# Four-layer image kernel: output projection folded into the value weights, denominators by DMA, half-height copies of left-over channels in the patch stage

## The chip, the cores and the metric

The kernel runs on one core of a Trainium2 chip. The metric is the device time of one execution in microseconds (us), taken as the median of several runs. Everything is computed in float32. Engines are called as in the profile: PE (matrix), PEld (its weight loads), DVE (vector), ACT (scalar), POOL (GpSimd) and SP (which here only issues DMAs).

## What is computed

One image `x` of 48 channels and 128 x 128 pixels goes through four layers, each of the form `x = x + layer(groupnorm(x))`. The change touches layers 0 and 2.

```python
# layer 0: attention over all 16384 pixels, one head of 48 channels
qkv = einsum('bchw,oc->bohw', x, qkv_w)            # 1x1
qkv = depthwise_conv3x3(qkv, dw_w)                 # SAME
q, k, v = split(qkv, 3);  q, k = l2norm(q), l2norm(k)
attn = softmax(einsum('bnc,bmc->bnm', q, k) * temperature)
out = einsum('bnm,bmc->bnc', attn, v)
return einsum('bchw,oc->bohw', out, proj_w)        # the projection

# layer 1: four sweeps of a recurrent 5-tap convolution over rows and columns
# layer 2: the patch stage
hidden = conv1x1(x, w_hidden)                      # 48 -> 288
q, k, v = split(depthwise_conv3x3(hidden, w_dw), 3)
out = irfft2(rfft2(patches(q)) * rfft2(patches(k)))   # 8x8 patches
return conv1x1(v * layernorm_over_channels(out), w_out)
# layer 3: a state-space scan over 4096 tokens of 192 channels
```

## The kernel before

The four layers run one after the other, with the image held in two large SBUF tiles, `xa` and `xb`. Instructions are placed by a scheduler that keeps every dependence; where the source uses the wrapper `InOrder` (ACT and PE in most stages), the order is the one in which the source writes them.

**Layer 0, first part (`attention`).** The 1x1 product and the 3x3 convolution are one matrix product: the weights of `l0_w` and `l0_dw` are multiplied into a tile `wt` (L106 `packed_weights`), whose 128 partitions hold 64 channels of one image row and 64 of the next, and whose last plane takes the left-over channels from a tile `rest`. In `wt` the columns 0 to 127 make q and k and the columns 128 to 191 make v. The groupnorm statistics of `x` (32 `bn_stats`, L155) come first; then bands of 16 rows are normalised, copied by DMA and convolved. Each token's v is turned by PE and stored in `v`, 64 columns per token of which column 32 is set to one (L273), so that the sums below also give the softmax denominator.

**Layer 0, second part (`attend`).** For each of 32 chunks of 512 queries (`c`) and each of 64 key tiles (`j`, both halves of the keys at once), PE makes the scores in four 64 x 64 quarters (`scores`, 4 products), ACT takes the exponential (`e`), and PE sums `v` against it in four quarters (`sums`, 4 products into `acc`). The sums lag the scores by two tiles. PSUM holds three score buffers `s` and one `acc`. When a chunk's sums are complete, `Finish.__init__` copies `acc` to SBUF on ACT (`o`) and adds its halves on DVE (`osum`, L361). Six tiles later `Finish.result` runs: a PE product of `proj` (128 x 112) with `osum` into one of the three `s` buffers, which adds the two key halves, applies the projection and spreads the denominator row over 48 rows; an ACT copy `y`; a DVE reciprocal (L369), a product (L370), the residual added (L371), statistics for the next groupnorm (L372) and a store of 48 x 512 values to `x1` (L373). A second version, `attend_shifted`, stands in the other branch of an `If` and does not run at this temperature.

**Layer 2 (`patch_conv`).** The image is convolved in groups `g` of four rows (32 groups). `fill(r)` prepares eight rows from row `r`: a memset of ones, the normalised rows (`normalise`, L93), one DMA of 49 partitions that shifts the rows by one into the upper half of `xp` (L765), two DMAs of 15 partitions (L768) and six DMAs of 19 partitions (L778, three horizontal shifts for each of two halves) that copy the last 19 channels of the row below into `rest`. For each group, `columns(g)` does three PE products per row from `xp`, `others(g)` a fourth per row from `rest`: even rows read the lower half of `rest` (partitions 0 to 56), odd rows the upper half (64 to 120). After that come the Fourier products (`keys`, `queries`, `back`), the layer norm and gate, and `turn`/`leave`. `rest` has three buffers of eight rows of 130 values. `fill(0)` issues its six `rest` DMAs from ACT, all later fills from SP; `fill(0)` and `fill(8)` stand ahead of the loop, the others are called at every second group.

The kernel lets a DMA go only when the one that last used its completion semaphore has landed; eight such semaphores are used in turn, by SP and ACT together.

Of the kernel before, what the change touches and what calls it, by code (L numbers as in the profile page):

```python
# [19 lines left out]
F32 = mybir.dt.float32  # L20
# [6 lines left out]
C = 48  # L27
H = W = 128
N = H * W
CH = 512  # L30
GAP = 49
# [59 lines left out]
def normalise(nc, out, in_, stats):  # L91
    mean, rstd = stats
    nc.vector.tensor_scalar(out, in_, mean, rstd, ALU.subtract, ALU.mult)  # L93


def rows(ap, n=W):
    return ap.rearrange("c (r w) -> c r w", w=n)


def packed_weights(nc, pool, name, w, dw, cols):  # L100

    w1 = pool.tile([128, 4, cols], F32, name="w1")
# [11 lines left out]
def attention(ctx, tc, xq, other, x1, const, ins):  # L114


    nc = tc.nc
    ident, blk, st = const["ident"], const["blk"], const["st"]
# [3 lines left out]
    kv = ctx.enter_context(tc.tile_pool(name="l0_kv", bufs=1))  # L122

    k = other[:, 0:HALF]

    v = other[:, HALF:N].rearrange("p (t c) -> p t c", c=64)


    proj = kv.tile([128, 64 + C], F32, name="proj")
    nc.vector.memset(proj, 0.0)  # L130
    for b in (0, 64):
        nc.sync.dma_start(proj[b : b + GAP, 0:C], ins["l0_proj"])
        nc.vector.memset(proj[b + 32 : b + 33, 64:], 1.0)
    temp = kv.tile([128, 1], F32, name="temp")
    nc.sync.dma_start(temp, ins["l0_temp"].to_broadcast([128, 1]))

# [3 lines left out]
    absT = kv.tile([128, 1], F32, name="absT")  # L140
    nc.vector.tensor_mul(absT, temp, sgn)

    with ExitStack() as a:
        act, pe = InOrder(tc, nc.scalar), InOrder(tc, nc.tensor)
        wp = a.enter_context(tc.tile_pool(name="l0_w", bufs=1))
        sp = a.enter_context(tc.tile_pool(name="l0_a", bufs=2))
        ps = a.enter_context(tc.tile_pool(name="l0_aps", bufs=4, space=PSUM))
        ps2 = a.enter_context(tc.tile_pool(name="l0_aps2", bufs=2, space=PSUM))
        ps1 = a.enter_context(tc.tile_pool(name="l0_aps1", bufs=1, space=PSUM))


        wt = packed_weights(nc, wp, "wt", ins["l0_w"], ins["l0_dw"], 192)

        for i in range(NQ):
            nc.vector.bn_stats(st[:, i, :], xq[0:C, i * CH : (i + 1) * CH])  # L155
        stats = group_stats(nc, wp, ps2, const, name="pss")
# [5 lines left out]
        rests = [wp.tile([128, R, S], F32, name=f"rest{i}") for i in range(2)]  # L162
# [72 lines left out]
        def take(t0, p, pv):  # L235

            sqs, psss, nrms = [], [], []
            for n in range(2):
                sqs.append(sp.tile([128, CH], F32, name="sq"))
                act.activation(sqs[n], p[n], AF.Square)  # L240
            vt = sp.tile([128, CH], F32, name="vt")
            act.copy(vt, pv)

            for n in range(2):
                psss.append(ps2.tile([128, CH], F32, name="pss"))
                pe.matmul(psss[n], lhsT=blk, rhs=sqs[n], start=True, stop=True)
                nrms.append(sp.tile([128, CH], F32, name="nrm"))
                act.activation(nrms[n], psss[n], AF.Sqrt)
            pt = ps1.tile([128, 4, 2, 64], F32, name="pt")
            for i in range(4):  # L250
                pe.transpose(
                    pt[:, i].rearrange("t n c -> t (n c)"), vt[:, i * 128 : (i + 1) * 128], ident
                )
            kb = 64 * (t0 // HALF)
            tk = t0 % HALF
            left = []
            for n in range(2):
                nc.vector.tensor_scalar_max(nrms[n], nrms[n], 1e-12)
# [13 lines left out]
            nc.gpsimd.memset(k[kb + 32 : kb + 33, tk : tk + 2 * CH], 1.0)  # L272
            nc.gpsimd.memset(v[:, t0 // 128 : t0 // 128 + 8, 32:33], 1.0)  # L273
            return left

        cur = band(0)
# [17 lines left out]
    small = nc.values_load(absT[0:1, 0:1].bitcast(mybir.dt.int32))  # L294
    bits = int(np.float32(32.0).view(np.int32))
    with tc.If(small <= bits) as near:
        attend(tc, xq, k, v, x1, proj, absT, st, ins)
    with near.Else():
        attend_shifted(tc, xq, k, v, x1, proj, absT, ident, st, ins)


@with_exitstack
def attend(ctx, tc, xq, k, v, x1, proj, absT, st, ins):

# [4 lines left out]
    nc = tc.nc  # L309
# [40 lines left out]
    class Finish:  # L350


        def __init__(self, c, acc):
            self.c = c
            self.cols = slice(c * CH, (c + 1) * CH)
            self.xres = sp.tile([C, CH], F32, name="xres")
            nc.sync.dma_start(self.xres, ins["x"][:, self.cols])
            o = sp.tile([128, 2, CH], F32, name="o")
            act.copy(o, acc)
            self.o = sp.tile([128, CH], F32, name="osum")  # L360
            nc.vector.tensor_add(self.o, o[:, 0], o[:, 1])  # L361

        def result(self):
            p = ps_s.tile([128, 2, CH], F32, name="s")[0 : 64 + C, 0, :]
            pe.matmul(p, lhsT=proj, rhs=self.o, start=True, stop=True)
            y = sp.tile([64 + C, CH], F32, name="y")
            act.copy(y, p)
            rec = sp.tile([C, CH], F32, name="rec")
            nc.vector.reciprocal(rec, y[64 : 64 + C])  # L369
            nc.vector.tensor_mul(rec, y[0:C], rec)  # L370
            nc.vector.tensor_add(xq[0:C, self.cols], rec, self.xres)  # L371
            nc.vector.bn_stats(st[:, self.c, :], xq[0:C, self.cols])  # L372
            nc.sync.dma_start(x1[:, self.cols], xq[0:C, self.cols])  # L373

    waiting, finish, acc = [], None, None
    for c in range(NQ):
        for j in range(KT):
# [4 lines left out]
            while len(waiting) > BEHIND:  # L382
                n, i, e = waiting.pop(0)
# [10 lines left out]


@with_exitstack
def attend_shifted(ctx, tc, xq, k, v, x1, proj, absT, ident, st, ins):

    nc = tc.nc
    NQ = N // CH  # L400
# [11 lines left out]
    k16 = k16p.tile([128, HALF], F16, name="k16")  # L412
    for i in range(0, HALF, 2048):
        nc.vector.tensor_copy(k16[:, i : i + 2048], k[:, i : i + 2048])

    class Shift:

# [45 lines left out]
    class Finish:  # L463
# [9 lines left out]

        def result(self):
            p = ps_1.tile([128, CH], F32, name="pmisc")
            nc.tensor.matmul(p[0 : 64 + C], lhsT=proj, rhs=self.o, start=True, stop=True)
            rec = sp.tile([C, CH], F32, name="rec")
            nc.vector.reciprocal(rec, p[64 : 64 + C])
            nc.vector.tensor_mul(rec, p[0:C], rec)
            nc.vector.tensor_add(xq[0:C, self.cols], rec, self.xres)  # L480
            nc.vector.bn_stats(st[:, self.c, :], xq[0:C, self.cols])
            nc.sync.dma_start(x1[:, self.cols], xq[0:C, self.cols])
# [213 lines left out]
def patch_conv(ctx, tc, xq, other, const, ins):  # L696
# [42 lines left out]

    K1 = C + 1
    SP = W + 2
    RN = 8
# [5 lines left out]
    for at in (0, W + 1):  # L750
        nc.gpsimd.memset(xp[:, 1 : H + 1, at : at + 1], 0.0)
    stats = group_stats(nc, wp, ps_f, const, name="f")
    flat = xp.rearrange("c h w -> c (h w)")
    rests = [wp.tile([128, RN, SP], F32, name=f"rest{i}") for i in range(3)]

    def rest(y):

        return rests[(y + 1) // RN % 3][:, (y + 1) % RN, 0:W]

    def fill(r, queue=nc.sync):  # L760
        inside = xp[0:64, 1 + r : 1 + RN + r, 1 : W + 1]
        nc.gpsimd.memset(inside[32:64], 1.0)
        normalise(nc, inside[0:C], rows(xq[0:C, r * W : (r + RN) * W]), stats)
        new = slice(r + 1, r + 1 + RN)
        nc.sync.dma_start(xp[64 : 64 + K1, r : r + RN, :], xp[0:K1, new, :])  # L765
        lo, hi = max(r - 1, 0), H if r + RN == H else r - 1 + RN
        for n in range(2):
            nc.sync.dma_start(  # L768
                xp[64 * n + K1 : 64 * n + 64, lo:hi, :],
                xp[M * n : M * n + M, lo + 2 : hi + 2, :],  # L770
            )
        e = rests[r // RN % 3].rearrange("c h w -> c (h w)")
        size = KR // 3
        long = RN * SP - 2
        for n in range(2):
            for dx in range(3):
                at = 64 * n + size * dx
                queue.dma_start(  # L778
                    e[at : at + size, 0:long],
                    flat[2 * M : K1, (r + 1) * SP + dx : (r + 1) * SP + dx + long],  # L780
                )

    pcs, qkv, prod, lns, ys, yts = {}, {}, {}, {}, {}, {}
# [115 lines left out]
        dve.bn_stats(const["st"][:, g, :], xq[0:C, g * CH : (g + 1) * CH])  # L899

    NG = H // G
    fill(0, act)
    fill(RN)
    for g in range(NG + 3):

# [810 lines left out]
```

## Time and profile before

Three runs took 7662.93, 7664.13 and 7669.04 us; the median is 7664.13. The profiled execution took 7668.22 us, of which 7666.4 lie between the first and the last instruction (the span).

| stage (us of the span) | length | PE busy | what it is |
|---|---|---|---|
| 0 to 43 | 43 | 0.7 | loads, statistics, first band of layer 0 |
| 43 to 254 | 211 | 200.5 | convolution of layer 0 |
| 254 to 3817 | 3563 | 3562.7 | `attend`, 32 chunks |
| 3817 to 3841 | 24 | 2.0 | last result, start of the sweeps |
| 3841 to 4508 | 667 | most | sweeps of layer 1 |
| 4508 to 4560 | 52 | 21.2 | start of the patch stage |
| 4560 to 4880 | 320 | 316.6 | patch stage, steady |
| 4960 to 7667 | 2707 | 1453.3 | scan of layer 3; DVE 2590.7 busy, POOL 2573.7 |

A row of the profile names the line, engine, operation, the tiles written and read, the shape, and the number of instructions that were merged into it. A float32 product appears as two instructions (two passes). The line numbers of products and of most ACT and DVE operations in ordered stages are those of the wrapper (L48), so these are followed by the names of their tiles. "Idle before <- X" is the time that an engine stood still before an instruction, and what ended it.

### The profile page before, as it was taken

The page shows a single profiled execution, that of the slowest core. Times are in us where ns is not written, and L with a number is a line of the kernel's source. Part 1 is how long each engine was busy: PE and PEld are TensorE (multiplying, and loading weights), DVE is VectorE, ACT ScalarE, POOL GpSimd, SP SyncE. Part 2 cuts the span into 40 slices and gives each one's busy share as a digit, 9 for nine tenths or more (in the row PEclk, how much of TensorE's full clock was granted, in tenths as well). Part 3 has the DMA queues.
Part 4 walks back from the last instruction along what each step waited for, and adds up shares of the span by engine and source line. Part 5 has one row for each costly group of instructions (what it writes and reads, how often), then busy time and mean ns, then how long its engine had stood idle before and what let it go on. Part 6 is the DMA issues. An engine that isn't in the chain of part 4 may idle for free. (4 is left out here: it accounts for less than half of the span.)

```text
span 7666.4 us, 202951 instructions
## 1 busy us (share of the span) xinstructions
PE 6186.0 (81%) x93744; PEld 3145.7 (41%) x93744; DVE 3353.1 (44%) x2435; ACT 4405.6 (57%) x4864; POOL 2793.6 (36%) x573
## 2 busy tenths in 40 slices
PE   7999999999999999999988879745545555554555
PEld 2333333333333333333367755434434333434444
DVE  8300000000000000000022234489999999999998
ACT  2566666666666666666625003366666666666665
POOL 1000000000000000000000022299999999999998
PEclk9999999999999999999999999866767666776666
DMA  5000000000000000000000001166556566666776
GB/s 76 10 3 3 3 2 3 3 3 2 3 3 2 3 3 3 2 3 3 6 1 17 1 27 50 31 168 165 158 161 164 152 161 155 164 158 162 181 178 152
DMA packets 167594, 488.77 MB, mean 64 GB/s; under 512 B 33568, under 2 KB 51968, under 8 KB 163984
## 3 DMA queue, kind: packets, MB, share of 16 engines
q1 hardware_dynamic: 160584, 469.79, 24.4%
q8 instruction: 736, 12.06, 0.7%
q10 hardware_dynamic: 6152, 5.92, 0.3%
q14 instruction: 122, 1.00, 0.0%
HBM read 428.82 MB, written 22.02 MB: 59 GB/s over the span
## 5 line engine op out<-in xcount | busy, mean ns | idle before, releaser
L48 ACT ACTIVATE e<-s,absT 128x1024 f32<-128x1024 f32 x2048 | 2279.4, 1115 | 1215.1 <-PE s L48 1215.0
L1471 POOL TENSOR_TENSOR h<-du,bt 128x3072 f32<-128x3072 f32 (+1 forms) x386 | 2559.8, 6670 | 94.5 <-DMA du<-rep 77.4
L48 PE MATMUL s<-xa,xb 49*64 49x512 f32 x16384 | 2127.7, 589 | 10.6 <-DVE xb L266 10.6
L48 PE MATMUL acc<-e,xb 64*64 64x512 f32 x16384 | 2123.6, 588 | 0.0
L1478 DVE TENSOR_TENSOR_SCAN h<-dA,carry,h 128x1024 f32<-128x1024 f32 x864 | 1939.8, 2324 | 46.1 <-ACT dA L48 31.2
L48 ACT ACTIVATE dA<-dt,a 128x1024 f32<-128x1024 f32 x1152 | 1287.2, 1118 | 873.8 <-DVE h L1478 864.6
L48 PE MATMUL y<-h,cw 128*32 128x48 f32 x49152 | 892.0, 245 | 930.6 <-issue 486.6
L361 DVE TENSOR_TENSOR osum<-o 128x512 f32<-128x512 f32 x32 | 22.2, 693 | 3114.2 <-ACT o L48 3114.2
L593 POOL MEMSET xa<- 48x128 f32 x1 | 0.3, 324 | 3560.3 <-PE acc L48 3560.3
L48 PEld LDWEIGHTS y<-h,cw 128*32 128x32 f32 x49152 | 802.8, 139 | 1059.7 <-issue 650.7
L48 PEld LDWEIGHTS s<-xa,xb 49*64 49x64 f32 x16384 | 624.8, 132 | 1152.1 <-issue 603.7
L48 PEld LDWEIGHTS acc<-e,xb 64*64 64x64 f32 x16384 | 627.1, 132 | 1135.0 <-issue 1112.4
L1478 DVE TENSOR_TENSOR_SCAN h<-dA,h 128x1024 f32<-128x1024 f32 x288 | 636.1, 2270 | 45.9 <-ACT dA L48 34.9
L48 PE MATMUL yz<-ev,sel 128*8 128x48 f32 x4096 | 192.7, 260 | 288.1 <-ACT ev L48 283.1
L48 PEld LDWEIGHTS yz<-ev,sel 128*8 128x8 f32 x4096 | 162.4, 106 | 345.6 <-ACT ev L48 321.7
L657 PE MATMUL p<-xb,w 112*112 112x129 f32 x1524 | 236.4, 291 | 41.9 <-DVE xb L48 41.8
L657 PE MATMUL p<-xa,w 112*112 112x129 f32 x1524 | 232.2, 288 | 41.9 <-DVE xa L48 41.9
L678 POOL TENSOR_TENSOR xb<-xb,xa 48x2048 f32<-48x2048 f32 (+2 forms) x10 | 44.6, 4460 | 562.3 <-DVE xa L48 562.3
L657 PEld LDWEIGHTS p<-xb,w 112*112 112x112 f32 x1524 | 184.3, 179 | 93.8 <-DVE xb L48 93.8
L640 ACT COPY xa<-xb 48x128 f32<-48x128 f32 x256 | 107.4, 420 | 197.3 <-issue 138.8
L369 DVE RECIPROCAL rec<-y 48x512 f32<-48x512 f32 x32 | 107.1, 3348 | 257.7 <-ACT y L48 257.7
L657 PEld LDWEIGHTS p<-xa,w 112*112 112x112 f32 x1524 | 180.6, 176 | 93.3 <-DVE xa L48 93.3
(182 smaller groups left out, 3474.8 us busy)
## 6 DMA issues: line engine op xcount, KB each, us to landing
du<-rep SPq DMA_DIRECT2D x768, 256.0 KB
dt<-rep SPq DMA_DIRECT2D x768, 256.0 KB
rest<-xa SPq DMA_DIRECT2D x90, 77.0 KB
rest<-band SPq DMA_DIRECT2D x48, 129.9 KB
rep<-dd SPq DMA_DIRECT2D x24, 192.0 KB
yd<-ys ACTq DMA_DIRECT2D x256, 12.0 KB
band<-band SPq DMA_DIRECT2D x8, 414.4 KB
xa<-xa SPq DMA_DIRECT2D x16, 199.1 KB
```

The source lines that it names most:

```text
L48: ins = method(*args, **kwargs).ins
L361: nc.vector.tensor_add(self.o, o[:, 0], o[:, 1])
L369: nc.vector.reciprocal(rec, y[64 : 64 + C])
L593: nc.gpsimd.memset(b[64:K, lines, E + W - 1 : E + W], 0.0)
L640: nc.scalar.copy(u[at : at + C, :, y], t[0:C, E + h, E : E + W])
L657: nc.tensor.matmul(p, lhsT=w[0:K, which, i, :], rhs=state[0:K, 2 * i : 2 * i + L], start=False, stop=(i == 2),)
L678: nc.gpsimd.tensor_add(xr, xr, u[0:C, x : x + xr.shape[2], E : E + H].rearrange("c w h -> c h w"),)
L1471: nc.gpsimd.tensor_mul(h[:, p, ks], du.unsqueeze(1).to_broadcast([128, ks.stop - ks.start, LC]), r["bt"][:, ks],)
L1478: nc.vector.tensor_tensor_scan(h[:, p, k, :], dA, h[:, p, k, :], carry[:, i, k : k + 1] if ci else 0.0, ALU.mult, ALU.add,)
```

## The change

In layer 0 the projection moves from the end of the attention to its weights. Once, at the start, the value columns of `wt` are turned by PE, multiplied by `proj` (now 64 x 64) and written back. The v of each token then is already projected; its columns 48 to 63 (sixteen of them) are set to one instead of column 32. In `Finish` the PE product and the ACT copy are gone; DVE copies the second key half down (`second`), adds it (`y`), takes the reciprocal of 32 rows, and three DMAs of 16 partitions spread the sixteen equal denominator rows over 48 rows (`recs`). `result` keeps two DVE operations, the statistics and the store.

In the patch stage `rest` holds, for each half, only the rows of the parity that `others` reads from that half: four rows of 128 values in place of eight of 130. The six DMAs therefore read every second row (runs of 128 values). The first fill is made in two parts, rows 0 to 4 (its `rest` DMAs on ACT) and rows 5 to 7 (all on SP).

```diff
-    proj = kv.tile([128, 64 + C], F32, name="proj")
+    proj = kv.tile([64, 64], F32, name="proj")
     nc.vector.memset(proj, 0.0)
-    for b in (0, 64):
-        nc.sync.dma_start(proj[b : b + GAP, 0:C], ins["l0_proj"])
-        nc.vector.memset(proj[b + 32 : b + 33, 64:], 1.0)
+    nc.sync.dma_start(proj[0:GAP, 0:C], ins["l0_proj"])
...
         wt = packed_weights(nc, wp, "wt", ins["l0_w"], ins["l0_dw"], 192)
+        values = wt[:, :, 128:192]
+        turned = wp.tile([64, 4, 128], F32, name="turned")
+        pt = ps1.tile([128, 4, 2, 64], F32, name="pt").rearrange("c t n o -> c t (n o)")
+        for t in range(4):
+            pe.transpose(pt[0:64, t, :], values[:, t, :], ident)
+        act.copy(turned, pt[0:64])
+        pt = ps1.tile([128, 4, 2, 64], F32, name="pt")
+        for t in range(4):
+            pe.matmul(pt[:, t, 0, :], lhsT=turned[:, t, :], rhs=proj, start=True, stop=True)
+        act.copy(values, pt[:, :, 0, :])
...
-            nc.gpsimd.memset(v[:, t0 // 128 : t0 // 128 + 8, 32:33], 1.0)
+            nc.gpsimd.memset(v[:, t0 // 128 : t0 // 128 + 8, C:64], 1.0)
...
             act.copy(o, acc)
-            self.o = sp.tile([128, CH], F32, name="osum")
-            nc.vector.tensor_add(self.o, o[:, 0], o[:, 1])
+            both = sp.tile([128, CH], F32, name="both")
+            nc.vector.tensor_add(both, o[:, 0], o[:, 1])
+            second = sp.tile([64, CH], F32, name="second")
+            nc.vector.tensor_copy(second, both[64:128])
+            self.y = sp.tile([64, CH], F32, name="y")
+            nc.vector.tensor_add(self.y, both[0:64], second)
+
+            rec = sp.tile([64, CH], F32, name="rec")
+            nc.vector.reciprocal(rec[32:64], self.y[32:64])
+            self.rec = sp.tile([C, CH], F32, name="recs")
+            for i in range(0, C, 64 - C):
+                nc.sync.dma_start(self.rec[i : i + 64 - C], rec[C:64])
 
         def result(self):
-            p = ps_s.tile([128, 2, CH], F32, name="s")[0 : 64 + C, 0, :]
-            pe.matmul(p, lhsT=proj, rhs=self.o, start=True, stop=True)
-            y = sp.tile([64 + C, CH], F32, name="y")
-            act.copy(y, p)
-            rec = sp.tile([C, CH], F32, name="rec")
-            nc.vector.reciprocal(rec, y[64 : 64 + C])
-            nc.vector.tensor_mul(rec, y[0:C], rec)
-            nc.vector.tensor_add(xq[0:C, self.cols], rec, self.xres)
+            y = self.y[0:C]
+            nc.vector.tensor_mul(y, y, self.rec)
+            nc.vector.tensor_add(xq[0:C, self.cols], y, self.xres)
...
-    rests = [wp.tile([128, RN, SP], F32, name=f"rest{i}") for i in range(3)]
+    rests = [wp.tile([128, RN // 2, W], F32, name=f"rest{i}") for i in range(3)]
...
-    def fill(r, queue=nc.sync):
+    def fill(r, first=0, end=RN, queue=nc.sync):
...
-        nc.sync.dma_start(xp[64 : 64 + K1, r : r + RN, :], xp[0:K1, new, :])
-        lo, hi = max(r - 1, 0), H if r + RN == H else r - 1 + RN
+        nc.sync.dma_start(xp[64 : 64 + K1, r + first : r + end, :], xp[0:K1, at, :])
+        lo, hi = max(r - 1 + first, 0), H if r + end == H else r - 1 + end
...
         for n in range(2):
+            own = range(first + (first + n + 1) % 2, end, 2)
             for dx in range(3):
-                at = 64 * n + size * dx
+                to = 64 * n + size * dx
                 queue.dma_start(
-                    e[at : at + size, 0:long],
-                    flat[2 * M : K1, (r + 1) * SP + dx : (r + 1) * SP + dx + long],
+                    e[to : to + size, own.start // 2 : own.start // 2 + len(own), :],
+                    xp[2 * M : K1, r + 1 + own.start : r + 1 + end : 2, dx : dx + W],
                 )
...
-    fill(0, act)
+    fill(0, 0, G + 1, act)
+    fill(0, G + 1)
     fill(RN)
```

`attend_shifted` gets a small matrix that adds the key halves in place of `proj`; it does not run here.

More of the change, by code (lines that the diff above doesn't have):

```diff
@@ L296, in attention, with attend @@
     with tc.If(small <= bits) as near:
-        attend(tc, xq, k, v, x1, proj, absT, st, ins)
+        attend(tc, xq, k, v, x1, absT, st, ins)
     with near.Else():
-        attend_shifted(tc, xq, k, v, x1, proj, absT, ident, st, ins)
+        attend_shifted(tc, xq, k, v, x1, absT, ident, st, ins)
 @with_exitstack
-def attend(ctx, tc, xq, k, v, x1, proj, absT, st, ins):
+def attend(ctx, tc, xq, k, v, x1, absT, st, ins):
     nc = tc.nc
@@ L396, in attend_shifted @@
 @with_exitstack
-def attend_shifted(ctx, tc, xq, k, v, x1, proj, absT, ident, st, ins):
+def attend_shifted(ctx, tc, xq, k, v, x1, absT, ident, st, ins):
     nc = tc.nc
@@ L414, in attend_shifted @@
         nc.vector.tensor_copy(k16[:, i : i + 2048], k[:, i : i + 2048])
+    add = sp.tile([128, 64 + C], F32, name="add")
+    nc.vector.memset(add, 0.0)
+    for b in (0, 64):
+        nc.vector.tensor_copy(add[b : b + C, 0:C], ident[b : b + C, b : b + C])
+        nc.vector.tensor_copy(
+            add[b + 32 : b + 64, 64:], ident[b + 32 : b + 64, b + C : b + C + 1].to_broadcast([32, C])
+        )
     class Shift:
@@ L475, in result @@
             p = ps_1.tile([128, CH], F32, name="pmisc")
-            nc.tensor.matmul(p[0 : 64 + C], lhsT=proj, rhs=self.o, start=True, stop=True)
+            nc.tensor.matmul(p[0 : 64 + C], lhsT=add, rhs=self.o, start=True, stop=True)
             rec = sp.tile([C, CH], F32, name="rec")
@@ L752, in patch_conv @@
     stats = group_stats(nc, wp, ps_f, const, name="f")
-    flat = xp.rearrange("c h w -> c (h w)")
-    rests = [wp.tile([128, RN, SP], F32, name=f"rest{i}") for i in range(3)]
+    rests = [wp.tile([128, RN // 2, W], F32, name=f"rest{i}") for i in range(3)]
     def rest(y):
-        return rests[(y + 1) // RN % 3][:, (y + 1) % RN, 0:W]
-    def fill(r, queue=nc.sync):
-        inside = xp[0:64, 1 + r : 1 + RN + r, 1 : W + 1]
+        return rests[(y + 1) // RN % 3][:, (y + 1) % RN // 2, :]
+    def fill(r, first=0, end=RN, queue=nc.sync):
+        at = slice(1 + r + first, 1 + r + end)
+        inside = xp[0:64, at, 1 : W + 1]
         nc.gpsimd.memset(inside[32:64], 1.0)
-        normalise(nc, inside[0:C], rows(xq[0:C, r * W : (r + RN) * W]), stats)
-        new = slice(r + 1, r + 1 + RN)
-        nc.sync.dma_start(xp[64 : 64 + K1, r : r + RN, :], xp[0:K1, new, :])
-        lo, hi = max(r - 1, 0), H if r + RN == H else r - 1 + RN
+        normalise(nc, inside[0:C], rows(xq[0:C, (r + first) * W : (r + end) * W]), stats)
+        nc.sync.dma_start(xp[64 : 64 + K1, r + first : r + end, :], xp[0:K1, at, :])
+        lo, hi = max(r - 1 + first, 0), H if r + end == H else r - 1 + end
         for n in range(2):
@@ L771, in fill @@
             )
-        e = rests[r // RN % 3].rearrange("c h w -> c (h w)")
+        e = rests[r // RN % 3]
         size = KR // 3
-        long = RN * SP - 2
         for n in range(2):
+            own = range(first + (first + n + 1) % 2, end, 2)
             for dx in range(3):
-                at = 64 * n + size * dx
+                to = 64 * n + size * dx
                 queue.dma_start(
-                    e[at : at + size, 0:long],
-                    flat[2 * M : K1, (r + 1) * SP + dx : (r + 1) * SP + dx + long],
+                    e[to : to + size, own.start // 2 : own.start // 2 + len(own), :],
+                    xp[2 * M : K1, r + 1 + own.start : r + 1 + end : 2, dx : dx + W],
                 )
```

## The prediction

> **What bounds the kernel now.** I read the table of stretches first, because the stages have different limits.
>
> ```profile
> core 0: us, PE busy (x) PEld busy (x) DVE busy (x) ACT busy (x) POOL busy (x), PEclk, DMA share, GB/s
> 254.00:3817.00 3563.00, 3562.66 (x32830) 1260.33 (x32830) 189.10 (x156) 2323.53 (x2112) 1.27 (x2) 1.00 0.01 3
> 4508.00:4560.00 52.00, 21.15 (x77) 14.04 (x76) 17.78 (x29) 3.43 (x10) 3.17 (x5) 0.67 0.22 68
> 4560.00:4880.00 320.00, 316.55 (x1670) 188.02 (x1670) 135.63 (x279) 96.17 (x229) 83.90 (x84) 0.99 0.15 42
> ```
>
> In the attention PE has no idle time in 3563 us, while ACT is free a third and DVE nearly all of it: whatever leaves PE shortens the stage, and what DVE gains is hidden. The steady patch stage is also PE's. Its start is not: PE works 21 of 52 us.
>
> Second, the timeline of PE and ACT around one chunk's result (the weight loads left out):
>
> ```profile
> 375.63 1.05 PE L48 MATMUL s<-xa,xb 49*64 49x512 f32 x8
> 376.49 1.05 PE L48 MATMUL acc<-e,xb 64*64 64x512 f32 x8
> ...
> 377.48 1.11 PE L48 MATMUL s<-osum,proj 128*112 128x512 f32 x2
> 378.52 1.09 PE L48 MATMUL s<-xa,xb 49*64 49x512 f32 x8
> ...
> 378.63 0.59 ACT L48 COPY y<-s 112x512 f32<-112x512 f32 x1 [0.70 <-PE s L48]
> ...
> 379.43 1.04 PE L48 MATMUL acc<-e,xb 64*64 64x512 f32 x8
> ...
> 380.29 1.04 PE L48 MATMUL s<-xa,xb 49*64 49x512 f32 x8
> ```
>
> A group starts 0.86 us after the one before; one key tile (scores and sums) takes 1.72. Scores that would have started at 377.35 start at 378.52, because the projection stands between them.
>
> Third, the end of the attention, where no next chunk covers anything:
>
> ```profile
> 3817.09 1.01 ACT L48 COPY o<-acc 128x1024 f32<-128x1024 f32 x1 [1.38 <-PE acc L48]
> ...
> 3818.97 1.32 PE L48 MATMUL s<-osum,proj 128*112 128x512 f32 x2 [1.95 <-DVE osum L361]
> ...
> 3820.34 0.59 ACT L48 COPY y<-s 112x512 f32<-112x512 f32 x1 [2.23 <-PE s L48]
> 3820.95 3.35 DVE L369 RECIPROCAL rec<-y 48x512 f32<-48x512 f32 x1 [2.12 <-ACT y L48]
> ...
> 3825.82 0.31 SPq L373 DMA_DIRECT2D x<-xa  x1
> ```
>
> Fourth, PE's timeline at the start of the patch stage, and the DMA queues in two windows (packets, MB, share of 16 engines): 4532 to 4547, and 4511.8 to 4512.5, where SP's queue moves the 512-byte rows of `fm`.
>
> ```profile
> 4523.17 7.58 PE L48 MATMUL pc<-wt,xa 128*128 128x288 f32 x24 [10.04 <-DMA xa<-xa]
> 4530.68 0.75 PE L48 MATMUL pc<-wt,rest 57*128 57x288 f32 x2
> 4547.23 2.26 PE L48 MATMUL pc<-wt,rest 57*128 57x288 f32 x6 [15.79 <-DMA rest<-xa]
> 4549.41 8.12 PE L48 MATMUL pc<-wt,xa 128*128 128x288 f32 x24
> 4557.46 1.24 PE L48 MATMUL pc<-wt,rest 57*128 57x288 f32 x8
> ...
> 4561.23 6.09 PE L48 MATMUL pc<-wt,xa 128*128 128x288 f32 x24
> ```
> ```profile
> q1 hardware_dynamic: 83, 0.33, 6.7%
> q10 hardware_dynamic: 48, 0.19, 3.1%
> ```
> ```profile
> q1 hardware_dynamic: 139, 0.06, 31.0%
> ```
>
> The first row of group 0 has its left-over channels in time, the second waits 15.79 us for a `rest` DMA. In that window the two queues together use 9.8% of sixteen engines, about one and a half, and until 4545 the rate stays near 26 GB/s.
>
> **What the Trainium skill says.** "DMA: Bandwidth & Descriptors", section "Why a DMA increments its semaphore by 16 and not by 1": a DMA is spread over the largest number of engines up to 16 that divides its slowest dimension. That dimension is 19 for `rest`, so one engine; 49 gives seven, 15 fifteen. The trace agrees: 77 KB per DMA at 26 GB/s is 3.0 us each, 18 us per fill, all on one engine. Its section "Issuing engines are not separate DMA queues" says that DMAs of ACT and SP run on the same engines; the trace agrees, since ACT's second three `rest` DMAs, issued by 4523.65, land at 4547, shared with fill(8)'s from SP. "TensorEngine Tiling (Array Packing)", section "Key Properties", says that a change of tiling mode drains PE; the 0.3 us around the projection beyond its streaming agree. "TensorE: Matmul & The Clock Gate", section "What's actually happening", says PE runs at half clock after idling; the trace agrees, with 7.58 and 8.12 us where a warm group of 24 takes 6.09.
>
> **Part 1, the result in the chunks.** The projection products start at 488.88, 600.16, and so on to 3716.00, always 111.28 us apart. Sixty-four tiles at 1.72 are 110.08. The rest, 1.20 us, is the projection: two passes of 0.43 and 0.34 of drain and refill. It occurs 31 times inside the stream: 31 x 1.20 = 37.2 us gone. What could be late next: ACT needs 64 x 1.115 + 1.0 = 72 us of a chunk's 110, and loses the `y` copy; the accumulator's copy `o` stays as it is. DVE's new work per chunk (0.69 + 0.4 + 0.69 + 3.35 + 3 x 0.69, about 7.2 us) and four SP DMAs lie in 110 us in which both are idle; `result` waits for the `recs` DMAs on DVE, behind which nothing of PE's or ACT's depends. Removing work from a stream without gaps can't gain less than the two passes, 26.5 us, nor more than 38.
>
> **Part 2, the last result.** From the end of `o` (3818.10) to the store's issue (3825.82) is 7.7 us. The new chain: add 0.69, copy 0.4 (nearest row: a one-source DVE operation on 128x512 SBUF values, 0.435), add 0.69, reciprocal 3.35 (fewer partitions, same 512 columns), three issues at about 0.37 and a landing, product and residual 0.68 each, and six handovers of 0.05. For the landing no row shows a 32 KB copy within SBUF; the bands' DMA at the start ended 3.1 us before PE used it (39.81 to 42.91), and no landing can cost under about 1.5 with issue and transfer; I take 2. Sum 9.5, so +1.8 (bounds +1 to +3).
>
> **Part 3, the start of layer 0.** Four transposes, an ACT copy, four products, an ACT copy of 128x256: at most 6 us from 12.8 (end of the `wt` product on DVE) or from 14 (landing of `proj`). PE is idle until 31.28 (the statistics) and the convolution starts at 42.91. DVE's `bn_stats` hide it. Taken as 0; if ACT's copies delayed the square root of the statistics, +2. The wider POOL memset (0.12 before, 8 elements to 128 per partition) precedes sums that start 6 us later: 0.
>
> **Part 4, the start of the patch stage.** Anchor: group 1's fourth products end at 4558.70, PE warm. In the changed kernel these need, on the one engine, all `rest` DMAs of fill(0) and fill(8). Their packets are rows of 512 bytes: rows 1, 3 and 0, 2, 4 in the first part (5 x 3 x 19 = 285), the other three rows (171) and fill(8) (8 x 3 x 19 = 456), together 912, where before they were 228 packets of 4152 bytes at 158 ns (26 GB/s). What does a 512-byte packet cost? SP's queue above: 31.0% of 16 x 0.7 us over 139 packets is 25 ns, 31 of them only completion markers, so nearly 28 for a full one. With many engines busy at once (the chunk loads of the scan, 6353.0 to 6355.5) the same division gives 45. Sources here are rows of 520 bytes pitch, less well placed than `fm`'s; I take 30, bounds 25 and 45. Then 27.4 us, plus this engine's share of the 49- and 15-partition DMAs (7 rows of 2600, 1560 and 4160 bytes, about 2.3, and 0.6): 30.3 from a first packet at about 4515.8, so 4546.1, and the products of the last row 0.6. PE itself could be there at 4539 (start 4519.5, then 7.6 + 2.3 + 8.1 + 1.2), so it waits some 7 us before the last row and is cold again, which costs about 3 us (the cold excess seen from 4547 to 4557.5). Gain: 4558.7 - 4549.7 = 9. At 25 ns 13.6; at 45 a loss of 5. If only PE bound it, 20.
>
> **Part 5, the steady patch stage.** Two groups take 2 x 10.89 = 21.8 us of PE. The engine's work per fill goes from 18 + 1.6 to 456 x 0.030 + 1.6 = 15.3 us. Nothing gained, since PE binds; a single 2.8 us wait on `rest` at 4690.77 may go. SP issues as many DMAs as before and six more in the first fill. The scan follows the last row unchanged.
>
> **Sum.** -37.2 + 1.8 + 0 - 9.0 = -44.4 on a span of 7666.4. The profiled execution (7668.22) is 4.1 above the median; the difference is applied to the median: 7664.1 - 44.4 = 7619.7.
>
> **Rivals.** (a) *Small packets are dear*: at 40 to 45 ns the patch stage's start gains nothing or loses a little, and only the attention's 35.4 remain: 7629 to 7640, say 7632. For it: the 45 measured under load. Against: this engine is alone in these windows. (b) *The patch start is bound by PE only*: at most 20 + 2.8 gained, 7606. For it: DMAs may overlap more; against: 912 packets on one engine. (c) *The engine becomes the bound of the patch stage*, the one case of a slower kernel: from (21.8 - 1.6) / 456 = 44 ns per packet every fill is late; each ns above costs 15 fills x 0.456 = 6.8 us, and 0.9 at the start. The gain of 35.4 is used up at 48 ns; at 60 the sum is -35.4 + 108 + 18, 7755. For it: four times as many packets on one engine, and 45 under load; against: 28 measured. (d) That the projection's slot is not won because its buffer or DVE's new work holds something: nothing waits for DVE in the attention, so I give it no case of its own.
>
> **How the numbers follow.** Forecast 0.68, (a) 0.16, (b) 0.08, (c) 0.08. A run tells a change from none beyond 0.2%, 15 us. Forecast, (b) and nearly all of (a) are faster: 0.91. The part of (c) between 46 and 50 ns and the end of (a) fall within 15 us: 0.03; the rest of (c) is slower: 0.06. The forecast's own range is 7610 to 7630; with (a) and (b) taken in, 7606 to 7637.
>
> **What would show it.** Starts of equal tiles of successive chunks 110.08 us apart, no `osum` product. Store of the last chunk some 9.5 us after the end of `o`. In the patch stage PE's wait in group 0 under 4 us and one of 5 to 10 at group 1's last row, group 1 done near 4547 when counted from the same start of the stage; packets of 512 bytes near 30 ns; no waits on `rest` afterwards. I am wrong if chunks stay above 111 us, if PE waits for `rest` at every second group, or if the convolution of layer 0 starts later than 43.

## The result, and the profile after

Five runs of the changed kernel took 7623.17 to 7633.47 us, median 7626.9; five of the kernel before, taken together with them, 7662.93 to 7669.04, median 7667.98. The ratio is 0.9949, 95% interval [0.9934, 0.9963]: 41 us less, where 44.4 had been forecast. The profiled execution of the changed kernel took 7623.17 us (span 7621.4) and is the fastest of its five. Cut at the same instructions in both profiles, the spans differ like this:

| stage | before | after | difference | forecast |
|---|---|---|---|---|
| start to the end of the last `o` copy | 3818.11 | 3780.80 | -37.3 | -37.2 |
| end of that `o` to the first product of the sweeps | 23.08 | 37.52 | +14.4 | +1.8 |
| sweeps | 666.9 | 667.6 | +0.7 | 0 |
| patch stage (last sweep product to the square root of the token statistics) | 420.8 | 403.1 | -17.8 | -9 |
| scan, to the end | 2737.5 | 2732.4 | -5.1 | 0 |

The total is close to the forecast because two terms of it were off by about 12.6 and 8.8 in opposite directions. The scan's 5.1 is no effect: in the ten runs below, which leave its code alone, its length lies between 2725.7 and 2739.4. The sweeps spread in the same way, 664.0 to 667.8.

The table of stretches of the changed kernel, to be held against the one shown of before (columns as there: the stretch, its length, busy time of PE, its weight loads, DVE, ACT and POOL, granted clock, share of the DMA engines, GB/s):

```profile
core 0: us, PE busy (x) PEld busy (x) DVE busy (x) ACT busy (x) POOL busy (x), PEclk, DMA share, GB/s
254.00:3780.00 3526.00, 3525.36 (x32768) 1300.07 (x32768) 223.20 (x218) 2305.46 (x2082) 1.32 (x3) 1.00 0.02 4
4486.00:4523.00 37.00, 18.43 (x72) 12.68 (x76) 18.44 (x30) 2.53 (x9) 2.86 (x5) 0.77 0.29 82
4523.00:4850.00 327.00, 325.85 (x1722) 194.21 (x1724) 140.42 (x289) 98.86 (x234) 86.79 (x87) 0.99 0.13 32
```

PE still has no idle time in the attention, but 62 products fewer (32768 in place of 32830: two passes for each of 31 chunks). The slot of the projection is gone, as the timeline of the changed kernel after the second chunk begins shows:

```profile
371.24 0.42 DVE L370 COPY second<-both 64x512 f32<-64x512 f32 x1
...
375.79 1.78 SPq L378 DMA_DIRECT2D recs<-rec  x3
...
377.46 1.04 PE L48 MATMUL s<-xa,xb 49*64 49x512 f32 x8
378.32 1.04 PE L48 MATMUL acc<-e,xb 64*64 64x512 f32 x8
...
379.06 0.68 DVE L382 TENSOR_TENSOR y<-y,recs 48x512 f32<-48x512 f32 x1 [3.30 <-DMA recs<-rec]
379.18 1.04 PE L48 MATMUL s<-xa,xb 49*64 49x512 f32 x8
```

Scores follow scores by 1.72 us straight through the stretch in which DVE and the `recs` DMAs make the result; the `o` copies of successive chunks are 110.08 us apart. Note the copy `second`: 0.42 us. At the end of the attention the same instruction reads differently:

```profile
3779.79 1.01 ACT L48 COPY o<-acc 128x1024 f32<-128x1024 f32 x1 [1.40 <-PE acc L48]
...
3780.22 13.91 POOL L610 MEMSET xb<- 32x16512 f32 x1
3780.83 0.69 DVE L368 TENSOR_TENSOR both<-o 128x512 f32<-128x512 f32 x1 [97.39 <-ACT o L48]
3781.56 12.85 DVE L370 COPY second<-both 64x512 f32<-64x512 f32 x1
...
3794.44 0.68 DVE L372 TENSOR_TENSOR y<-both,second 64x512 f32<-64x512 f32 x1
...
3803.32 0.31 SPq L385 DMA_DIRECT2D x<-xa  x1
```

It takes 12.85 us and ends 0.28 us after POOL's memset of the sweeps' borders (3794.13). No bracket stands behind it: the profile counts the time as work, not as a wait. The addition `both`, which runs beside the same memset, takes its usual 0.69. That memset was in the kernel before too, beside the sum `osum`, and harmed nothing there (kernel before, timeline of POOL and DVE):

```profile
3817.12 13.92 POOL L589 MEMSET xb<- 32x16512 f32 x1 [1.21 <-PE acc L48]
3818.14 0.69 DVE L361 TENSOR_TENSOR osum<-o 128x512 f32<-128x512 f32 x1 [94.81 <-ACT o L48]
```

Third, PE's timeline at the start of the patch stage of the changed kernel, whose last sweep product ends at 4485.91 (4508.08 before):

```profile
4498.52 8.06 PE L48 MATMUL pc<-wt,xa 128*128 128x288 f32 x24 [7.48 <-DVE xa L93]
4506.51 1.24 PE L48 MATMUL pc<-wt,rest 57*128 57x288 f32 x8
4507.74 6.09 PE L48 MATMUL pc<-wt,xa 128*128 128x288 f32 x24
4513.76 1.24 PE L48 MATMUL pc<-wt,rest 57*128 57x288 f32 x6
4521.65 1.30 PE L48 MATMUL pc<-wt,rest 57*128 57x288 f32 x2 [6.66 <-DMA rest<-xa]
4522.88 1.56 PE L48 MATMUL f<-qkv,fm 64*64 64x384 f32 x8
...
4526.84 7.57 PE L48 MATMUL pc<-wt,xa 128*128 128x288 f32 x24
4534.34 1.24 PE L48 MATMUL pc<-wt,rest 57*128 57x288 f32 x8
```

The 15.79 us wait in group 0 is gone; one of 6.66 stands at group 1's last row, and after it PE runs `f` and the columns of group 2 slowly (1.56 and 7.57 us; warm, at the full clock, they are 0.88 and 6.09; the granted clock from 4522.9 to 4534.3 is 0.69). The DMA queue in the window 4510 to 4516 (packets, MB, share of 16 engines):

```profile
q1 hardware_dynamic: 249, 0.13, 7.1%
```

In 6 us 249 packets passed, almost all of 512 bytes: one every 24.1 ns. Their lengths add up to 7.1% of 16 x 6 = 6.8 us, 27 ns each, so they overlap. I had priced them at 30.

Counting the end of each group's fourth products from the last sweep product, the changed kernel is 13.6 us ahead at group 1, 10.7 at group 2 and every group to 12, 14.9 at group 13 and 17.2 from group 14 on. The second step is the stall in the middle of the stage, of which the kernel before shows:

```profile
4690.77 1.29 PE L48 MATMUL pc<-wt,rest 57*128 57x288 f32 x2 [2.79 <-DMA rest<-xa]
4691.99 1.56 PE L48 MATMUL f<-qkv,fm 64*64 64x384 f32 x8
```

A wait of 2.79 us cost 6.4 us (17.2 - 10.8): 4.1 by the end of that row's products, and 2.3 in the products after it, which run slowly (`f` 1.56 in place of 0.88; the granted clock from 4690.7 to 4697.5 is 0.54).

### The profile page after: what moved, and what is told of

Its sections match the earlier page's. It is cut to its first block, busy times and chain, and to the rows that moved or that the text cites. A ratio compares the mean times of both kernels' runs of the same rounds, so it can differ in the third digit from the quotient of the medians.

```text
span 7621.4 us, 203064 instructions
## 1 busy us (share of the span) xinstructions
PE 6122.5 (80%) x93692; PEld 3175.4 (42%) x93692; DVE 3399.7 (45%) x2498; ACT 4389.3 (58%) x4835; POOL 2795.3 (37%) x574
## 5 line engine op out<-in xcount | busy, mean ns | idle before, releaser
L368 DVE TENSOR_TENSOR both<-o 128x512 f32<-128x512 f32 x32 | 22.2, 692 | 3192.2 <-ACT o L48 3192.2
L48 PEld LDWEIGHTS s<-xa,xb 49*64 49x64 f32 x16384 | 650.4, 132 | 1122.9 <-issue 583.3
L48 PEld LDWEIGHTS acc<-e,xb 64*64 64x64 f32 x16384 | 649.7, 132 | 1112.4 <-issue 1089.5
L678 PE MATMUL p<-xa,w 112*112 112x129 f32 x1524 | 234.5, 290 | 41.1 <-DVE xa L48 41.0
L48 PE MATMUL pc<-wt,xa 128*128 128x288 f32 x768 | 198.3, 416 | 7.5 <-DVE xa L93 7.5
```

What stands on the lines that cost most here:

```text
L48: ins = method(*args, **kwargs).ins
L368: nc.vector.tensor_add(both, o[:, 0], o[:, 1])
L678: nc.tensor.matmul(p, lhsT=w[0:K, which, i, :], rhs=state[0:K, 2 * i : 2 * i + L], start=False, stop=(i == 2),)
```

## The experiments

Ten kernels ran. All are edits of the changed kernel but the one with the patch stage alone. The stages are cut as above, from each run's profiled execution.

| run | median us | ratio to before | last `o` to sweeps | sweeps | patch stage | scan |
|---|---|---|---|---|---|---|
| changed kernel | 7626.9 | 0.9949 [0.9934, 0.9963] | 37.5 | 667.6 | 403.1 | 2732.4 |
| `second` as a maximum | 7611.27 | 0.9930 [0.9917, 0.9944] | 25.5 | 664.8 | 403.8 | 2733.1 |
| memset in eight | 7608.66 | 0.9925 [0.9912, 0.9939] | 21.2 | 664.4 | 405.3 | 2739.4 |
| attention only | 7641.44 | 0.9967 [0.9955, 0.9979] | 37.5 | 666.7 | 419.9 | 2735.8 |
| patch stage only | 7647.61 | 0.9979 [0.9970, 0.9987] | 22.6 | 664.8 | 403.8 | 2733.8 |
| half rows only | 7620.52 | 0.9942 [0.9926, 0.9959] | 37.8 | 666.8 | 400.0 | 2733.5 |
| division only | 7640.21 | 0.9968 [0.9955, 0.9980] | 37.8 | 667.0 | 418.5 | 2738.8 |
| second fill divided too | 7622.36 | 0.9945 [0.9928, 0.9961] | 37.5 | 667.8 | 396.0 | 2736.7 |
| all three remedies | 7596.01 | 0.9912 [0.9895, 0.9928] | 20.8 | 667.1 | 396.1 | 2725.7 |
| all rows, row by row | 7693.72 | 1.0040 [1.0025, 1.0054] | 37.7 | 666.7 | 469.5 | 2734.2 |
| second part on ACT | 7619.09 | 0.9943 [0.9926, 0.9959] | 37.7 | 664.0 | 402.8 | 2728.2 |

### What held the copy at the end of the attention

The Trainium skill, "SBUF — State Buffer", section "Who interferes with whom", says that VectorE and GpSimd share one pair of ports, which one instruction takes for its whole length while the other blocks; that copies in the two-port mode need it; and that an operation with two SBUF inputs contends only with a GpSimd instruction that reads SBUF. "VectorE: DVE Perf Modes", section "The perf-mode tier table (the rule you actually need)", gives a float32 copy the doubled mode and `tensor_tensor` the single one. The trace's 0.42 against 0.69 us for the same 512 columns fits that. So the two-input form should pass a memset, and the copy should not.

```diff
-            nc.vector.tensor_copy(second, both[64:128])
+            nc.vector.tensor_tensor(second, both[64:128], both[64:128], op=ALU.max)
```

> The move of `second` is written as the maximum of both[64:128] with itself, the rest as in the changed kernel. Theory (the copy's fast mode needs a port that GpSimd holds through its 13.9 us memset of xb; a two-input operation does not need it): the last chunk's operation takes about 0.7 us in place of 12.85, the end of `o` to the store's issue comes to 10 to 10.5 us in place of 22.5, and the time falls by about 12 to 7611 to 7615. Rival 1 (any DVE operation that moves values from partitions 64 to 127 down to 0 to 63 is held up beside that memset): still about 13 us, 7623 to 7628. Rival 2 (the copy waits for something that the profile doesn't show, in the program's order of that place): still about 13 us.

The timeline of that run:

```profile
3781.73 13.91 POOL L610 MEMSET xb<- 32x16512 f32 x1
3782.34 0.69 DVE L368 TENSOR_TENSOR both<-o 128x512 f32<-128x512 f32 x1 [97.13 <-ACT o L48]
3783.07 0.69 DVE L370 TENSOR_TENSOR second<-both 64x512 f32<-64x512 f32 x1
...
3792.67 0.31 SPq L385 DMA_DIRECT2D x<-xa  x1
```

Same place, same move between partitions, same memset beside it, and 0.69 us. From the end of `o` (3782.31) to the store's issue are 10.4 us in place of 22.5. Both rivals fall: they said 13 us. The second run keeps the copy and divides the memset:

```diff
-        nc.gpsimd.memset(b[32:64, lines, inside], 1.0)
+        for at in range(lines.start, lines.stop, 16):
+            nc.gpsimd.memset(b[32:64, at : at + 16, inside], 1.0)
```

> The ones in `borders` for xb are written in eight memsets of 16 lines in place of one of 128 lines; the copy `second` is as in the changed kernel. If the memset holds the port for a whole instruction and gives it up between two, the copy is held for the rest of one part only: at most 1.75 us more than its 0.42, so 0.5 to 2.2 us, and the time is 7612 to 7617. If GpSimd keeps it as long as it has the next memset queued, the copy still takes about 12 us and the time is 7623 to 7628. If the copy's length has nothing to do with the memset, it is 12.85 us as before.

```profile
3780.07 1.82 POOL L611 MEMSET xb<- 32x2064 f32 x1
3780.62 0.69 DVE L368 TENSOR_TENSOR both<-o 128x512 f32<-128x512 f32 x1 [97.42 <-ACT o L48]
3781.34 0.82 DVE L370 COPY second<-both 64x512 f32<-64x512 f32 x1
3781.94 0.37 POOL L598 MEMSET mask<- 128x129 f32 x1
```

Six of the eight parts have run earlier, under the last tiles of the attention; the copy meets the seventh. It is held for the rest of that part and ends (3782.16) 0.27 us after it (3781.89), the same distance as 0.28 in the changed kernel. POOL's next memset, of `mask`, starts 0.05 us after the part and takes 0.37 where it takes 0.21 in the changed kernel, which fits that POOL waited in its turn. So in this run the port was held for one instruction and given up between two. The time came out below the expected 7612 to 7617 for a reason that no theory of mine had: the sweeps' first product starts 2.6 us after ACT's first normalised slice in this run (3799.20 to 3801.80), where it starts 7.1 after it in the run with the maximum (3800.67 to 3807.81) and in the changed kernel. PE waits for two slices instead of six. The edited line serves xa as well as xb, so the later memset of xa is divided too (eight parts from 3806.9 on, too late to touch the copy). Which of the two divisions brings the earlier start, and what ties PE to the later slices when the memsets are whole, stays open.

### Do the parts add up

The attention alone, and then the patch stage alone (in the kernel before):

> The attention as in the changed kernel, the patch stage as before. If the parts add up: chunks 110.08 us apart (-37.2), last result +14.5, patch stage unchanged, so -23 on 7668: about 7645. If part of the gain in the patch stage came from the attention (addresses of buffers, state of the queues), it is below 7640.

> The patch stage as in the changed kernel, the attention as before. If the parts add up: from the last product of the sweeps to the end of the patch stage 17 to 18 us less, the scan unchanged: about 7650. By the prediction's size of this part (-9) it would be 7659. If the 5 us by which the scan differed between the two profiles belong to the change of the patch stage, it is 7645.

Attention alone is 24.5 us below the kernel before that was measured with it (7665.89), the patch stage alone 18.3: together 42.7, against 41.1 for both. Both times are some 2 to 4 us below what was expected, less than the scan varies between runs, so the stages decide. The stages concerned (the end of the attention, the patch stage) are as long as in the kernels that they were taken from, to about 1 us. The patch stage is really worth 17 to 18, not the 9 of the forecast, and the scan keeps its length without the change of the patch stage (2735.8) and with it (2733.8).

### What the patch stage gained from

The half rows alone, with the first fill made whole:

```diff
-    fill(0, 0, G + 1, act)
-    fill(0, G + 1)
+    fill(0, 0, RN, act)
```

> The changed kernel, but the first fill is made whole again (rows 0 to 7, its `rest` DMAs on ACT). Counted from the last product of the sweeps to the token statistics' square root, the patch stage takes 420.8 us before and 403.1 after. Theory (the gain comes from the work of one DMA engine, 912 packets at 29 ns in place of 228 at 158 ns, whichever way it is divided): the wait at group 1's last row stays, group 0 waits at most 2 us, 403 to 407, time 7627 to 7632. Rival (the division of the first fill is what brings it, by letting PE start at group 0 sooner): 412 or more, 7636 or more.

The division alone, with `rest` in whole rows:

```diff
-    rests = [wp.tile([128, RN // 2, W], F32, name=f"rest{i}") for i in range(3)]
+    rests = [wp.tile([128, RN, SP], F32, name=f"rest{i}") for i in range(3)]
...
-                    e[to : to + size, own.start // 2 : own.start // 2 + len(own), :],
-                    xp[2 * M : K1, r + 1 + own.start : r + 1 + end : 2, dx : dx + W],
+                    e[to : to + size, first * SP : first * SP + long],
+                    flat[2 * M : K1, (r + first + 1) * SP + dx : (r + first + 1) * SP + dx + long],
```

> The changed kernel, but `rest` holds whole rows of 130 values as before; the first fill is in two parts. Theory (bytes on the one engine decide): the three parts still need 36 us of that engine, so PE waits 10 us or more at group 1's last row in place of 6.7, and the single wait on `rest` of 2.8 us in the middle of the stage is back: patch stage 415 to 420, time 7639 to 7644. Rival (the division brings it): 407 or less, 7632 or less.

The half rows bring the gain: 420.8 to 400.0. The division is worth 1.4 on whole rows (419.9 to 418.5, attention alone against this run) and *costs* 3.0 on half rows (400.0 to 403.1); neither theory had that sign. Each of these is one profile, and four profiles with the changed patch stage lie between 403.1 and 405.3, so differences of this size are best read from the groups. By the end of group 2 those four are 8.8 to 10.7 us ahead of the kernel before; half rows alone is 14.3 ahead, and the division on whole rows 3.6 *behind*. In these profiles the division thus costs about 4 us at the start with either kind of row. PE's timeline with half rows only, last sweep product at 4485.36:

```profile
4499.41 7.78 PE L48 MATMUL pc<-wt,xa 128*128 128x288 f32 x24 [8.95 <-DVE xa L93]
...
4510.04 2.26 PE L48 MATMUL pc<-wt,rest 57*128 57x288 f32 x6 [2.17 <-DMA rest<-xa]
...
4520.37 1.34 PE L48 MATMUL pc<-wt,rest 57*128 57x288 f32 x8
4521.64 0.88 PE L48 MATMUL f<-qkv,fm 64*64 64x384 f32 x8
```

PE starts 1.4 us later and waits 2.17 in group 0, and then finds the left-over channels of row 8, which group 1's last row needs, already there (the expectation had said that this wait would stay and the stage be 403 to 407). So group 1 is done 36.3 us after the sweeps, against 37.0 with the division. With the division PE only reaches the same landing sooner, stands still for 6.66 in one piece, and then pays 1.56 + 1.56 + 7.57 - (0.88 + 0.88 + 6.09) = 2.8 us for the slower clock. One part of the expectation for the division alone failed as well: no wait on `rest` came back in the middle of the stage; its longest is 14.07 us, at group 1's last row. The half rows are therefore not the only way past that wait: in the kernel before the row landed 182.7 us after the sweeps, and with the division alone PE, by then 3.5 us behind, ends that row at 183.5. That it simply comes too late to wait fits these times; no run tests it.

What holds row 8? First I suspected SP's queue, which issues the second part's six `rest` DMAs ahead of the second fill:

```diff
-    fill(0, G + 1)
+    fill(0, G + 1, queue=act)
```

> The changed kernel with the second part's `rest` DMAs issued by ACT, behind the first part's, in place of SP. In the changed kernel SP issues these six from 4500.0 to 4504.8 and only then the bands of the second fill, and the one engine moves 28 packets between 4508 and 4510 where it moves 80 in other windows. Theory (SP's issuing holds back the second fill by some 3 to 5 us): PE's wait at group 1's last row falls from 6.7 to 2 to 4 us and the patch stage from 403 to 398 to 401; time 7619 to 7624. Rival (the engine's work alone sets it): the wait stays within 1 us of 6.7 and the stage within 1 us of 403.

```profile
4509.86 1.24 PE L48 MATMUL pc<-wt,rest 57*128 57x288 f32 x6
4517.80 1.30 PE L48 MATMUL pc<-wt,rest 57*128 57x288 f32 x2 [6.70 <-DMA rest<-xa]
```

The wait is 6.70, the stage 402.8: the rival was right, SP's queue is not what delays row 8. The time itself (7619.09) falls where my theory put it, but the difference lies in the sweeps and the scan, not in this stage. The engine's work decides: the last of the 912 packets starts 34.85 us after the sweeps in the changed kernel, 34.69 with the first fill whole and 34.55 here. Then the order of that work must count:

```diff
-    fill(RN)
+    fill(RN, 0, 2)
+    fill(RN, 2)
```

> The changed kernel with the second fill in two parts as well, rows 8 and 9 ahead of rows 10 to 15, so that row 8's left-over channels, which group 1's last row needs, are 57 packets behind the first fill and not 456. Theory (this wait is what is left of the start, with the slower clock after it): the 6.7 us wait goes, `f` and the columns of group 2 run at 0.88 and 6.09 us in place of 1.56 and 7.57, the patch stage is 6 to 9 us shorter (394 to 397), time 7618 to 7621. Rival (SP's queue, which now issues nine more DMAs, makes group 2's bands late): a wait of the same size on xa at group 2 and no gain.

```profile
4509.38 6.09 PE L48 MATMUL pc<-wt,xa 128*128 128x288 f32 x24
4515.40 1.24 PE L48 MATMUL pc<-wt,rest 57*128 57x288 f32 x8
4516.57 0.88 PE L48 MATMUL f<-qkv,fm 64*64 64x384 f32 x8
...
4519.17 6.09 PE L48 MATMUL pc<-wt,xa 128*128 128x288 f32 x24
```

The wait is gone, PE stays warm, and the stage is 396.0, 7.1 us shorter. SP's nine further DMAs cost two small waits on `rest`, 1.8 us together. The total (7622.36, just above what was expected) shows less of it, with a scan 4.3 us longer than in the changed kernel's profile; the stage is what this run tells.

### From where a fill by rows is too dear

The prediction's slower case was that the one DMA engine becomes the bound of the stage. All eight rows copied one by one double its packets:

```diff
-                    e[to : to + size, own.start // 2 : own.start // 2 + len(own), :],
-                    xp[2 * M : K1, r + 1 + own.start : r + 1 + end : 2, dx : dx + W],
+                    e[to : to + size, first:end, :],
+                    xp[2 * M : K1, r + 1 + first : r + 1 + end, dx : dx + W],
```

> The changed kernel, but `rest` holds all eight rows, still copied row by row in runs of 512 bytes: 912 packets for a fill in place of 456. This puts the one engine past the point from which the prediction's third rival decides. At 25 ns from one packet to the next (80 packets in 2 us, the densest windows of the changed kernel) a fill takes 22.8 + 1.6 = 24.4 us of the engine against PE's 21.8: 15 fills x 2.6 = 39 more, and 23 more at the start, so 7685 to 7695. At 29 ns (the mean length of a packet) it is 28.0 us: 93 and 26 more, so 7740 to 7750. If the engine doesn't bind the stage even then (the rests are spread or run ahead), only the start is longer: 7645 to 7655.

The patch stage is 469.5, 66.4 more, near the 62 of the first reckoning (23.8 of it by group 2, where 23 were reckoned); the time, 7693.72, is slower than before (1.0040 [1.0025, 1.0054]). In 4604 to 4616 its queue shows 490 packets, one every 24.5 ns, so the engine is full, and PE waits:

```profile
PE pc L48 <- DMA rest<-xa: 43.9, 8, 16.4
```

(waits by engine and releaser in the patch stage: us in total, times, the longest; the changed kernel has one, of 6.7). The changed kernel stands on the safe side of that mechanism only because each half copies every second row: 456 packets take 11 us of the engine, 912 take 22.3 (24.1 and 24.5 ns each) and the bands' share comes on top, while PE needs 21.8 for two groups.

### The version that the runs point to

The maximum, the memset in eight parts and the divided second fill together:

> The move of `second` as a maximum, the ones for xb in eight memsets and the second fill in two parts, together. If the three effects add up: 12 for the copy, 4 for the earlier start of the sweeps that the run with the memset in parts showed, 6 to 9 for the second fill, so 22 to 25 less than the changed kernel: 7601 to 7605. If the gains share a wait, it is above 7608.

The median is 7596.01, ratio 0.9912 [0.9895, 0.9928], faster than both kernels (the interval lies wholly below the changed kernel's, [0.9934, 0.9963]). Up to the token statistics its profile is 24.9 us ahead of the changed kernel's (4864.10 against 4888.98): 16.8 at the end of the attention and 7.0 in the patch stage. So the gains add up, as 22 to 25 us had been expected; that the time is below the expected 7601 to 7605 lies in a scan of 2725.7, within its spread.

## Why the prediction was right, and where its terms were not

- **Part 1** (-37.2) was right in mechanism and size: -37.3, chunks 110.08 apart. Nothing took the projection's place on PE; DVE and ACT had the room that the forecast counted.
- **Part 2** (+1.8) is the step that failed. Its term "copy 0.4 (nearest row: a one-source DVE operation on 128x512 SBUF values, 0.435)" measured 12.85 in this one place, and the store was issued 22.5 us after the end of `o`, not 9.5. The duration was right for a copy alone, 0.42 in the other chunks. I had taken a price from a row without asking what runs beside it on POOL; the memset stood in the profile of before, harmless since a two-input addition was its neighbour. The rule on the shared ports, cited above, was not part of that reckoning. There is a slip in the sum as well: its terms add up to 9.9, not 9.5, so +2.2. Without the lock that is good: the maximum gives 25.5 against 23.08, +2.4, and the `recs` landing, which no row of before showed, came 3.3 us after its first issue where 3.1 was assumed.
- **Part 3** (0) was right: the convolution of layer 0 starts at 43.18 in place of 42.91. By the letter that crosses the sign "later than 43", but in the profiles of the ten experiments it starts between 42.4 and 43.3 (42.5 with the attention as before), so no delay is shown.
- **Part 4** (-9) had the mechanism right, the one engine and 912 packets, a single wait at group 1's last row (6.66, forecast 5 to 10) and a cold, slow PE after it. The mis-sized term is the packet: taken as 30 ns, it is 27 long and follows its neighbour by 24. The row of `fm` already gives 27: of its 139 packets 17 are markers, and the 31 that were subtracted belong to both queues. So the engine's part, forecast as 30.3 us, took 25.4 (first left-over packet at 4495.38, last at 4520.75). Two smaller terms went the other way: the first packet started 9.5 us after the sweeps and not 7.7, and PE went on 0.9 after the start of the last. Row 8 lands 35.7 us after the sweeps in place of the forecast 38.0, and the start gains 10.7. Here the length of a packet was mistaken for its spacing.
- **Part 5** (0, "a single 2.8 us wait on `rest` at 4690.77 may go") was the larger miss of the stage. The wait did go, and was worth 6.4, since the slow clock after it counts too. In part 4 that cost was in the sum; here it was forgotten.
- **The rivals.** (a) falls, as packets are not dear. (b) said 20 + 2.8 for a start bound by PE alone; with the second fill divided too, the stage gains 24.9 (18.3 at the start, 6.4 by the wait in the middle), so its size was reachable, but not with this change. (c) is real in mechanism, and double the packets bring it out, but at 24 ns the changed kernel's packets take 11 us of the 20.2 that PE leaves them.

So the total came out right by luck, through a loss of 12.6 us that was not foreseen and a gain of 8.8 that was not counted. Parts 1 and 3 and the mechanism of part 4 are borne out by the lengths of their own stages; the agreement of the sum proves nothing.

## What to carry to other kernels

Before a DVE copy is added on a path without cover, look at what POOL does at that time: beside a long memset a float32 copy waited for its end (12.85 us), the two-input form of the same copy did not (0.69), and dividing the memset helped as well (0.82). A stall of PE costs its length and the slow clock after it, so a wait is better removed by ordering the transfers (the rows needed first, first) than by letting PE reach it sooner. For small packets on one DMA engine count the spacing, not the length, and compare packets per fill with the time that PE gives the fill.

## What the runs showed of the hardware beyond that

- POOL's memset of 32 x 16512 values (13.91 us), which only writes, held a DVE float32 copy for 12.4 us, while a reciprocal and additions ran beside it at their usual length (before: `osum` 0.69, reciprocal 3.35). The held time is booked as DVE busy.
- 512-byte packets within SBUF on one engine: one every 24 to 25 ns, 20 to 21 GB/s; the 4152-byte packets of the kernel before ran at 26.
- A PE stall of 2.79 us cost 6.4 us in all; one of 6.66 us cost some 2.8 beyond its length.
